# A graph attention layer and a graph transformer layer: head groups outermost, layer 0 and the output projection between attention rounds, seven equal query blocks

## The chip, the core and the metric

The kernel runs on one core of one Trainium2 chip. The metric is the device time of one execution in microseconds (us), the median of several. PE is the matrix engine (PEld its weight loads), DVE the vector engine, ACT the scalar (activation) engine, POOL the GpSimd engine, and SP the engine that only issues DMAs here. Matrix products land in PSUM, all else lives in SBUF; DRAM is reached by DMA.

## The reference

There are N = 3,327 nodes with D = 128 features and a dense N x N matrix `adj` of zeros and ones, about a quarter of a per cent of them ones, the diagonal set.

```python
# layer 0: graph attention, one head
H = x @ W.T + b;  s = H @ a_s;  r = H @ a_r
e = leaky_relu(A * s + A * r.T, 0.2)
x = layernorm(x + softmax(where(A > 0, e, NEG), axis=1) @ H)
# layer 1: D = 128 heads of width h = 8, every head sees all nodes
q, k, v = ((x @ Wq.T).reshape(d, n, h), ...)
a = softmax(einsum('dnh,dmh->dnm', q, k) * d**-0.5 + adj + adj, axis=2)
x = layernorm(x + einsum('dnm,dmh->dnh', a, v).reshape(n, h*d) @ Wo.T)
```

The 128 heads of layer 1 have 3,327 x 3,327 scores each, 1.4 billion exponentials. The reshape gives head d the rows d x 3,327 onward of the flat q, k and v, so a head is a contiguous stretch of some 26 consecutive nodes' projections: the first heads need only the first rows of x after layer 0.

## The kernel before

**Layer 0 (L99 to L225).** x is loaded and turned, h = x W, r is spread over all partitions (`rb`), s is a column (`scol`). Then 26 row tiles of 128 nodes follow, each with a row block of adj of 128 x 3,327 elements. Per tile DVE checks that adj holds zeros and ones only (L176), forms (r + s) x adj (L179) and the leaky ReLU (L182); POOL makes the mask (L183); DVE adds it and takes the row maximum (L185); ACT takes the exponential (L192); PE turns the result in 26 pieces (L198), DVE and ACT copy the pieces out (L203), PE multiplies by h (L209), and DVE divides, adds x (L214) and collects the statistics (L218, L219). At the end come a square root on ACT for all tiles (L221) and the normalization (L225).

**q, k, v (L242 to L263).** Per tile there are two matmuls of 512 columns each for q, k and v. ACT rounds q and k to a short format (L243), DVE makes the remainder (L244), so q and k have a high and a low half, and DVE takes their largest magnitude (L247). SP stores all to DRAM (`qT`, `kT`, `vd`) (L251, L263). Then a flag is computed: only if all scores are small enough and adj is zeros and ones does the fast path `plain()` run, which takes no row maximum; otherwise the slow `shifted()`.

**Attention (`plain`).** Heads go in 32 groups of four. Query columns go in blocks: six of 512 and one of 256. The outer loop is over the blocks, the inner over the groups: `groups = [(g, b) for b in blocks for g in range(NG)]`. For each block the adjT columns are loaded once on POOL's queue as bf16 (`at`, L290), and ACT makes exp(2 adj) of every third key tile (`ft`, L333). For each group and block, q (`q4b`, L346), k (`k4b`, L350) and v (`v4b`, L354) are loaded by SP, so k and v come 7 times in all for each group.

Keys are in 26 tiles (key = partition x 26 + tile). A group and block has 26 **rounds**. A round makes two half tiles of scores on PE (L298, four small matmuls, one per head). Of three consecutive key tiles one is a *times* tile: ACT takes the exponential of the scores directly from PSUM (L420) and POOL multiplies by exp(2 adj) (L421). For the other two DVE adds adj to the scores (L428) and ACT takes the exponential later for all four heads at once (L395, 2,048 elements). The last two key tiles are both added ones. Four rounds later (`LAG`) PE multiplies by v (L370, eight instructions into one PSUM bank for four heads), the ninth column of v being ones, which gives the denominator. After the last key tile DVE copies the sums out (L379) and SP stores them to `oT` (L382). There are three score buffers in PSUM of two banks each and two for the sums.

PE, ACT and DVE run in the order in which the program issues (a manual schedule); POOL and SP are ordered by the compiler's own scheduler.

**Output (L572 to L598).** For each row tile SP loads 9 x 128 values per node from `oT`, DVE divides (L572, L573), PE turns (L580), DVE and ACT copy (L582), PE multiplies by Wo (L585), and the residual and the normalization follow (L587 to L595).

Of the kernel before, what the change touches and what calls it, by code (L numbers as in the profile page):

```python
# [8 lines left out]
F32 = mybir.dt.float32  # L9
# [5 lines left out]
AX = mybir.AxisListType  # L15

# [5 lines left out]
NB = 512  # L22

SAFE = 20.0


def _ap(t, offset, dims):
    return bass.AP(tensor=t.tensor, offset=t.offset + offset, ap=[list(d) for d in dims])


@with_exitstack
def kernel(
# [20 lines left out]

    nc = tc.nc
# [11 lines left out]

    blocks = []
    for n0 in range(0, N, NB):
        nb = min(NB, (N - n0 + 1) // 2 * 2)
        at = min(n0, N - nb)  # L70
        blocks.append((at, nb, n0 - at))
    HG = 4
    NG = D // HG

# [9 lines left out]
    oT = dram.tile([H1, G], F32, name="oT")  # L84

    ident = const.tile([P, P], F32, name="ident")
    make_identity(nc, ident)
    x1 = const.tile([P, NT, D], F32, name="x1")
# [3 lines left out]

    seen = const.tile([P, 3, NT], F32, name="seen")
    nc.vector.memset(seen, 0.0)
    flag = const.tile([1, 1], I32, name="flag")

    def load_rows(engine, dst, src):

        engine.dma_start(dst[:, :FULL, :], src[: FULL * P, :].rearrange("(t p) d -> p t d", p=P))  # L99
        engine.dma_start(dst[:LAST, FULL, :], src[FULL * P :, :])  # L100


    with ExitStack() as l0:
        big = l0.enter_context(tc.tile_pool(name="l0_big", bufs=1))
        xsb = big.tile([P, NT, D], F32, name="xsb")
        load_rows(nc.sync, xsb, x)
        w0 = big.tile([P, D], F32, name="w0")
        nc.scalar.dma_start(w0, w0T)
        bcol = big.tile([P, 1], F32, name="bcol")
        nc.scalar.dma_start(bcol, b0)  # L110
        ascol = big.tile([P, 1], F32, name="ascol")
        nc.scalar.dma_start(ascol, a_s)
        arcol = big.tile([P, 1], F32, name="arcol")
        nc.scalar.dma_start(arcol, a_r)
        wq = big.tile([P, H * D], F32, name="wq")
        nc.scalar.dma_start(wq, wqT.rearrange("k h c -> k (h c)"))
        wk = big.tile([P, H * D], F32, name="wk")
        nc.scalar.dma_start(wk, wkT.rearrange("k h c -> k (h c)"))
        wv = big.tile([P, D * H], F32, name="wv")
        nc.scalar.dma_start(wv, wvT.rearrange("k c h -> k (c h)"))  # L120
        nc.scalar.dma_start(wo, woT)

        ones = big.tile([1, H1], F32, name="ones")
        nc.vector.memset(ones, 1.0)
        nc.gpsimd.dma_start(vd[G : G + 1, :], ones)

        xT = big.tile([P, N], F32, name="xT")
        hT = big.tile([P, N], F32, name="hT")
        hsb = big.tile([P, NT, D], F32, name="hsb")
        rb = big.tile([P, N], F32, name="rb")  # L130
        scol = big.tile([P, NT], F32, name="scol")

        ps = l0.enter_context(tc.tile_pool(name="l0_ps", bufs=4, space=bass.MemoryType.PSUM))
        ps1 = l0.enter_context(tc.tile_pool(name="l0_ps1", bufs=2, space=bass.MemoryType.PSUM))

        def transpose_rows(src, dst):

            for t0 in range(0, NT, 4):
                ts_ = range(t0, min(NT, t0 + 4))
                pt = ps.tile([P, 512], F32, tag="mm", name="pt")  # L140
                w = 0
                for t in ts_:
                    nc.tensor.transpose(pt[:, w : w + rows[t]], src[: rows[t], t, :], ident[: rows[t], : rows[t]])
                    w += rows[t]
                nc.vector.tensor_copy(dst[:, t0 * P : t0 * P + w], pt[:, :w])

        transpose_rows(xsb, xT)
        for n0 in range(0, N, 512):
            nb = min(512, N - n0)
            ph = ps.tile([P, 512], F32, tag="mm", name="ph")  # L150
            nc.tensor.matmul(ph[:, :nb], w0, xT[:, n0 : n0 + nb], start=True, stop=True)
            nc.vector.tensor_scalar(hT[:, n0 : n0 + nb], ph[:, :nb], bcol, None, op0=ALU.add)
            pr = ps.tile([P, 512], F32, tag="mm", name="pr")
            nc.tensor.matmul(pr[:, :nb], arcol.to_broadcast([P, P]), hT[:, n0 : n0 + nb], start=True, stop=True)
            nc.scalar.copy(rb[:, n0 : n0 + nb], pr[:, :nb])
        for t in range(NT):
            r = rows[t]
            pb = ps.tile([P, 512], F32, tag="mm", name="pb")
            nc.tensor.transpose(pb[:r, :D], hT[:, t * P : t * P + r], ident)
            nc.tensor.matmul(pb[:r, D : D + 1], hT[:, t * P : t * P + r], ascol, start=True, stop=True)  # L160
            nc.vector.tensor_copy(hsb[:r, t, :], pb[:r, :D])
            nc.scalar.copy(scol[:r, t : t + 1], pb[:r, D : D + 1])

        mv = big.tile([P, NT, 2], F32, name="mv")
        nc.vector.memset(mv, 1.0)
        with ExitStack() as gat:
            ap_ = gat.enter_context(tc.tile_pool(name="gat_a", bufs=2))
            wp = gat.enter_context(tc.tile_pool(name="gat_w", bufs=1))
            tp = gat.enter_context(tc.tile_pool(name="gat_t", bufs=2))
            sp = gat.enter_context(tc.tile_pool(name="gat_s", bufs=3))  # L170
            for t in range(NT):
                r = rows[t]
                a = ap_.tile([P, N], F32, name="a")
                nc.sync.dma_start(a[:r], adj[t * P : t * P + r, :])
                e = wp.tile([P, N], F32, name="e")
                nc.vector.scalar_tensor_tensor(  # L176
                    e[:r], a[:r], 0.0, a[:r], op0=ALU.is_gt, op1=ALU.not_equal, accum_out=seen[:r, 2, t : t + 1]
                )
                nc.vector.scalar_tensor_tensor(  # L179
                    e[:r], rb[:r], scol[:r, t : t + 1], a[:r], op0=ALU.add, op1=ALU.mult  # L180
                )
                nc.vector.scalar_tensor_tensor(e[:r], e[:r], ALPHA, e[:r], op0=ALU.mult, op1=ALU.max)  # L182
                nc.gpsimd.tensor_scalar(a[:r], a[:r], 0.0, NEG, op0=ALU.is_le, op1=ALU.mult)  # L183
                mx = sp.tile([P, 1], F32, name="mx")
                nc.vector.tensor_tensor_reduce(  # L185
                    e[:r], e[:r], a[:r], 1.0, LOWEST, op0=ALU.add, op1=ALU.max, accum_out=mx[:r]
                )
                nm = sp.tile([P, 1], F32, name="nm")
                nc.vector.tensor_scalar_mul(nm[:r], mx[:r], -1.0)  # L189
                p = tp.tile([P, N], F32, name="p")  # L190
                den = sp.tile([P, 1], F32, name="den")
                nc.scalar.activation(p[:r], e[:r], AF.Exp, bias=nm[:r], scale=1.0, accum_out=den[:r])  # L192
                pT = tp.tile([P, NT, P], F32, name="pT")
                for i0 in range(0, NT, 4):
                    is_ = range(i0, min(NT, i0 + 4))
                    pp = ps.tile([P, 4, P], F32, tag="mm", name="pp")
                    for i in is_:
                        nc.tensor.transpose(pp[: rows[i], i - i0, :r], p[:r, i * P : i * P + rows[i]], ident[:r, :r])  # L198
                    copy = nc.vector.tensor_copy if (i0 // 4) % 2 else nc.scalar.copy
                    full = [i for i in is_ if rows[i] == P]  # L200
                    if full:
                        n = len(full)
                        copy(pT[:, i0 : i0 + n, :r], pp[:, :n, :r])  # L203
                    if len(full) < len(is_):
                        i = is_[-1]
                        copy(pT[: rows[i], i, :r], pp[: rows[i], i - i0, :r])
                po = ps1.tile([P, D], F32, name="po")
                for i in range(NT):
                    nc.tensor.matmul(  # L209
                        po[:r], pT[: rows[i], i, :r], hsb[: rows[i], i, :], start=(i == 0), stop=(i == NT - 1)  # L210
                    )
                rd = sp.tile([P, 1], F32, name="rd")
                nc.vector.reciprocal(rd[:r], den[:r])
                nc.vector.scalar_tensor_tensor(  # L214
                    x1[:r, t, :], po[:r], rd[:r], xsb[:r, t, :], op0=ALU.mult, op1=ALU.add
                )
                st = sp.tile([P, 6], F32, name="st")
                nc.vector.bn_stats(st[:r], x1[:r, t, :])  # L218
                nc.vector.bn_aggr(mv[:r, t, :], st[:r])  # L219
# [419 lines left out]
```

## Time and profile before

| | us |
|---|---|
| median of 3 runs | 12,036.66 (12,035.51 to 12,043.38) |
| the profiled execution, its own time | 12,038.34 |
| its span, first to last instruction | 12,036.6 |
| busy PE / DVE / ACT / POOL | 11,035 / 9,677 / 10,238 / 8,419 |
| mean granted PE clock | 0.908 of full |
| DMA | 727.9 MB, mean 60 GB/s |

The span is cut by what each stage issues. Layer 0 ends near 905 us, the q/k/v stage near 1,260; the first add of attention starts at 1,343. The six blocks of 512 columns start at about 1,343, 2,887, 4,433, 5,982, 7,529 and 9,077, the one of 256 at 10,619, the output at 11,900. In a list of groups a row has the line, engine, operation, output <- inputs, shapes and count, then total busy time and mean ns of one, then the engine's idle time before these and what ended it. A row of windows has start:end, length, and per engine the busy time with the number of instructions, then the granted clock, the share of DMA time and GB/s. A row of the timeline has start and duration in us first.

### The profile page before, as it was taken

The page shows a single profiled execution, that of the slowest core. Times are in us where ns is not written, and L with a number is a line of the kernel's source. Part 1 is how long each engine was busy: PE and PEld are TensorE (multiplying, and loading weights), DVE is VectorE, ACT ScalarE, POOL GpSimd, SP SyncE. Part 2 cuts the span into 40 slices and gives each one's busy share as a digit, 9 for nine tenths or more (in the row PEclk, how much of TensorE's full clock was granted, in tenths as well). Part 3 has the DMA queues.
Part 4 walks back from the last instruction along what each step waited for, and adds up shares of the span by engine and source line. Part 5 has one row for each costly group of instructions (what it writes and reads, how often), then busy time and mean ns, then how long its engine had stood idle before and what let it go on. Part 6 is the DMA issues. An engine that isn't in the chain of part 4 may idle for free.

```text
span 12036.6 us, 184261 instructions
## 1 busy us (share of the span) xinstructions
PE 11035.1 (92%) x73013; PEld 4269.1 (35%) x73013; DVE 9676.5 (80%) x9126; ACT 10238.2 (85%) x8026; POOL 8419.1 (70%) x3888
## 2 busy tenths in 40 slices
PE   3335599999999999999999999999999999999998
PEld 3332133333333333333333333333333333333334
DVE  5545488888888888888888888888888888866666
ACT  1112599999999999999999999999999999976664
POOL 3440487777787877778777878777877887765552
PEclk6668799999999999999999999999999999965556
DMA  1117211112111121111211111211111111111112
GB/s 70 51 40 228 63 55 53 52 53 63 55 53 53 54 62 56 52 54 55 62 55 52 54 55 53 63 53 54 55 52 58 54 55 52 53 58 61 59 61 82
DMA packets 373572, 727.90 MB, mean 60 GB/s; under 512 B 21360, under 2 KB 304574, under 8 KB 340701
## 3 DMA queue, kind: packets, MB, share of 16 engines
q1 hardware_dynamic: 343932, 690.00, 17.0%
q0 software_dynamic: 23888, 22.15, 1.2%
q8 instruction: 578, 9.47, 0.3%
q10 hardware_dynamic: 4880, 3.87, 0.1%
q14 instruction: 294, 2.41, 0.1%
HBM read 651.20 MB, written 86.87 MB: 61 GB/s over the span
## 4 chain that ended last, share of the span: by engine, by line
PE 74%; DVE 8%; DMA 5%; issue 3%; ACT 3%; SPq 1%; POOL 0%; another core or an unknown queue 0%; ACTq 0%; DVEq 0%; POOLq 0%
PE av L370 41%; PE scb L298 32%; DVE e L428 7%; DMA k4b<-kT 2%; ACT e L395 2%; DMA kT<-ksb 1%; ACT e L420 1%; SPq L251 1%; DMA vd<-vb 0%; PE py L585 0%; DMA o<-oT 0%; DMA q4b<-qT 0%; POOL a L183 0%; POOL e L421 0%
## 5 line engine op out<-in xcount | busy, mean ns | idle before, releaser
L428 DVE TENSOR_TENSOR e<-scb,at 128x1024 f32<-128x1024 f32 (+2 forms) x8064 | 8859.2, 1143 | 1774.5 <-PE scb L298 1529.4
L421 POOL TENSOR_TENSOR e<-e,ft 128x1024 f32<-128x1024 f32 (+1 forms) x3584 | 7968.6, 2224 | 2477.4 <-ACT e L420 1661.4
L395 ACT ACTIVATE e<-e 128x2048 f32<-128x2048 f32 (+1 forms) x4032 | 7298.9, 1810 | 196.4 <-DVE e L428 170.5
L370 PE MATMUL av<-e,v4b 128*32 128x512 f32 (+1 forms) x46592 | 6233.9, 610 | 3.5 <-ACT e L395 3.4
L298 PE MATMUL scb<-q4b,k4b 32*128 32x512 f32 (+2 forms) x23296 | 5057.8, 606 | 277.1 <-DMA k4b<-kT 201.7
L298 PEld LDWEIGHTS scb<-q4b,k4b 32*128 32x128 f32 (+1 forms) x23296 | 2882.1, 296 | 5510.6 <-DVE e L428 3053.3
L420 ACT ACTIVATE e<-scb 128x1024 f32<-128x1024 f32 (+1 forms) x3584 | 3515.6, 981 | 368.9 <-PE scb L298 365.3
L370 PEld LDWEIGHTS av<-e,v4b 128*32 128x32 f32 x46592 | 954.4, 112 | 1414.1 <-issue 1378.0
L183 POOL TENSOR_SCALAR a<-a 128x3327 f32<-128x3327 f32 (+1 forms) x26 | 385.3, 14819 | 498.6 <-DVE e L179 481.9
L198 PE MATMUL pp<-ident,p 128*128 128x128 f32 (+2 forms) x676 | 133.2, 383 | 567.9 <-ACT p L192 537.3
L192 ACT ACTIVATE p<-e,nm 128x3327 f32<-128x3327 f32 (+1 forms) x26 | 79.7, 3067 | 588.2 <-DVE nm L189 588.2
L198 PEld LDWEIGHTS pp<-ident,p 128*128 128x128 f32 (+2 forms) x676 | 125.9, 210 | 574.4 <-ACT p L192 542.2
L185 DVE CUSTOM_DVE_ANT_0 e<-e,a 128x3327 f32<-128x3327 f32 (+1 forms) x26 | 94.2, 3625 | 288.2 <-POOL a L183 288.2
L333 ACT ACT_TABLE_LOAD x1 | 1.3, 1283 | 206.8 <-DMA q4b<-qT 206.8
L256 POOL MEMSET vb<- 128x128 f32 x26 | 8.6, 330 | 240.8 <-DMA vd<-vb 180.4
L209 PE MATMUL po<-hsb,pT 128*128 128x128 f32 (+2 forms) x1352 | 157.0, 277 | 0.0
L379 DVE COPY o<-av 128x512 f32<-128x512 f32 (+1 forms) x224 | 144.4, 645 | 13.9 <-PE av L370 13.7
L209 PEld LDWEIGHTS po<-hsb,pT 128*128 128x128 f32 (+2 forms) x1352 | 155.4, 194 | 0.0
L203 ACT COPY pT<-pp 128x512 f32<-128x512 f32 (+1 forms) x104 | 52.6, 506 | 120.3 <-PE pp L198 119.5
L176 DVE SCALAR_TENSOR_TENSOR e<-a 128x3327 f32<-128x3327 f32 (+1 forms) x26 | 93.8, 3607 | 32.3 <-DMA a<-in_adj_dram 32.3
L290 POOL DMA_DIRECT2D at<-in_adjT_dram x14 | 14.7, 1054 | 148.7 <-DMA vd<-vb 126.6
L342 POOL MEMSET v4b<- 128x92 f32 x224 | 39.6, 177 | 107.7 <-PE av L370 86.9
(85 smaller groups left out, 1151.8 us busy)
## 6 DMA issues: line engine op xcount, KB each, us to landing
k4b<-kT SPq DMA_DIRECT2D x896, 415.9 KB
v4b<-vd SPq DMA_DIRECT2D x224, 468.0 KB
q4b<-qT SPq DMA_DIRECT2D x1536, 32.0 KB
a<-in_adj_dram SPq DMA_DIRECT2D x25, 1663.5 KB
qT<-qsb SPq DMA_DIRECT2D x50, 512.0 KB
kT<-ksb SPq DMA_DIRECT2D x50, 512.0 KB
at<-in_adjT_dram POOLq DMA_DIRECT2D x6, 2912.0 KB, 67.1
vd<-vb SPq DMA_DIRECT2D x25, 576.0 KB
```

What stands on the lines that cost most here:

```text
L183: nc.gpsimd.tensor_scalar(a[:r], a[:r], 0.0, NEG, op0=ALU.is_le, op1=ALU.mult)
L185: nc.vector.tensor_tensor_reduce(e[:r], e[:r], a[:r], 1.0, LOWEST, op0=ALU.add, op1=ALU.max, accum_out=mx[:r])
L198: nc.tensor.transpose(pp[: rows[i], i - i0, :r], p[:r, i * P : i * P + rows[i]], ident[:r, :r])
L209: nc.tensor.matmul(po[:r], pT[: rows[i], i, :r], hsb[: rows[i], i, :], start=(i == 0), stop=(i == NT - 1))
L251: nc.sync.dma_start(_ap(dst, half * H * G + t * P * D, [[D, r], [G, H], [1, D]]), sb[:r, half, :].bitcast(F32).rearrange("p (h c) -> p h c ...
L298: nc.tensor.matmul(dst, k4[32 * j : 32 * j + H4, i::NT], q4[32 * j : 32 * j + H4, :nb], start=True, stop=stop,)
L370: nc.tensor.matmul(s.av[32 * j : 32 * j + 32, : s.nb], s.v4[:r, j, i * H1 : i * H1 + 32], e[:r, j, : s.nb], start=(s.left == NT - 1), stop ...
L379: nc.vector.tensor_copy(o4[:, : s.nb], s.av[:, : s.nb])
L395: nc.scalar.activation(e, e, AF.Exp, scale=2.0)
L420: nc.scalar.activation(eh, x[:r, :, :nb], AF.Exp, scale=2.0)
L421: nc.gpsimd.tensor_tensor(eh, eh, f[:r, i // 3, :nb].unsqueeze(1).to_broadcast([r, 2, nb]), op=ALU.mult,)
L428: nc.vector.tensor_tensor(eh, x[:r, :, :nb], a[:r, i, :nb].unsqueeze(1).to_broadcast([r, 2, nb]), op=ALU.add,)
```

## The change

The fast path becomes one program, `special()`, in which all five engines follow the order of issue. It always runs; only when its flag says no does `general()`, the old way with `shifted()`, run after it.

- **Blocks.** Seven blocks of 476 columns (`NB` = 480, `WB` = 476); the last starts 5 columns early.
- **Order.** Groups are outermost, blocks inside: k and v are loaded once per group, halfway through the last block of the group before, q once per group and block.
- **adj.** It no longer stays in SBUF for a block. At the start POOL's queue copies adjT from DRAM to DRAM, as bf16 and in the order of use (`atd`); the factors exp(2 adj) = (e^2 - 1) adj + 1 are made by DVE and stored (`ftd`), for block 0 at the start, for blocks 1 to 6 during group 0. In attention both are streamed by SP for three rounds at a time, four such stretches ahead (`AHEAD`), in six buffers.
- **Layer 0, factored.** exp(leaky_relu(s + r)) divided by exp(s) is max(exp(0.2 r) t, exp(r)) with t = exp(-0.8 s). ACT computes the three vectors once, at the start. A tile then needs on DVE a tensor_scalar per key tile (`weigh`), a multiplication by adj > 0 (`mask`), and a check of adj (`count`), and on PE 26 products with h and a column of ones. There is no transpose, no maximum, and no exponential per tile.
- **Pieces.** Layer 0 of a tile, its q/k/v projection (evicted by DVE only) and the output projection of a tile are lists of small pieces (46 and 11). Tile 0 runs at the start. The tiles that group g + 1 reads are handled during group g, in its first three quarters; the output of tiles whose heads are complete follows after them. A piece is issued after a round whose number has reached its due value. The last tile's output comes at the end. The square root is an integer first guess and three Newton steps on DVE.
- **PSUM.** One bank for the pieces, one for the sums (there were two), six for scores as before. ACT does only attention's exponentials after the start.
- **Flag.** The bound on the scores comes from the norms of the weights' columns, not from q and k; it also asks that exp(r) and t are in range.

The diff cut to its core (the loops in `general` and `shifted` are the old ones):

```diff
-NB = 512
+NB = 480
+SAFE = 40.0
+AHEAD = 4
-            groups = [(g, b) for b in blocks for g in range(NG)]
+    NBLK = max(2, -(-N // NB))
+    WB = -(-N // (2 * NBLK)) * 2
+    blocks = [(min(b * WB, N - WB), b * WB - min(b * WB, N - WB)) for b in range(NBLK)]
+            def prepare(b, pool):
...
+                        nc.vector.tensor_scalar(f, f, E2 - 1.0, 1.0, op0=ALU.mult, op1=ALU.add)
+            def layer0(t):
...
+                    def weigh(c0, c1, n=n, i0=i0):
...
+                        for i in range(c0, c1):
+                            nc.vector.tensor_scalar(
+                                s["w"][:, i - i0, :r], s["t"][:, :r], ear[:, i : i + 1], er[:, i : i + 1],
+                                op0=ALU.mult, op1=ALU.max,
+                            )
+                    def mask(c0, c1, n=n, i0=i0):
+                        a, w = (v[:, c0 - i0 : c1 - i0, :r] for v in (s["a"][n], s["w"]))
+                        nc.vector.scalar_tensor_tensor(w, a, 0.0, w, op0=ALU.is_gt, op1=ALU.mult)
+                    def count(c0, c1, k, n=n, i0=i0):
...
+                        nc.vector.scalar_tensor_tensor(
+                            a, a, 0.0, a, op0=ALU.is_gt, op1=ALU.not_equal, accum_out=odd[:, t, k : k + 1]
+                        )
+                    def products(c0, c1, i0=i0, n=n):
...
+                        for i in range(c0, c1):
+                            nc.tensor.matmul(s["p"][:r, : D + 1], s["w"][: kr[i], i - i0, :r], hsb[: kr[i], i, :],
+                                start=(i == 0), stop=(i == NT - 1))
+                units += [finish, variance, root, scale, turn, keep_turned]
...
+                def high(dst, i, scale):
+                    s["hi"] = bg2.tile([P, 512], F32R, name="hi")
+                    nc.vector.tensor_scalar(s["hi"][:r], s["b"][:r], scale, None, op0=ALU.mult)
+                    store(dst, 0, i, s["hi"])
...
+                def divided(h0):
+                    o = s["o"]
+                    nc.gpsimd.tensor_tensor(
+                        o[:r, h0 : h0 + 4, :], o[:r, h0 : h0 + 4, :],
+                        o[:r, H, :].unsqueeze(1).to_broadcast([r, 4, D]), op=ALU.mult,
+                    )
...
+            def open_adj(b, n):
+                a = ap_.tile([P, 2, WB], BF16, name="at")
+                k = len(pairs_[n])
+                nc.sync.dma_start(a[:, :k, :], atd[b][n, :, :k, :])
+                f = None
+                if n < NTR:
+                    f = ap_.tile([P, WB], F32, name="ft")
+                    nc.sync.dma_start(f, ftd[b][n])
+                return a, f
...
+                for u in range(len(side)):
+                    if u < early:
+                        due[u] = u * (total // 4) // early
+                    elif u < before:
+                        lo = total // 4 if early else 0
+                        due[u] = lo + (u - early) * (total * 3 // 4 - lo) // (before - early)
+                    else:
+                        lo = min(max(total // 8, LAG + 2, due[before - 1] + 1 if before else 0), total - 1)
+                        due[u] = lo + (u - before) * (total - 1 - lo) // (len(side) - before)
...
+                        if n % 3 == 0:
+                            m = (g * NBLK + b) * NPR + n // 3
+                            want_adj(m + AHEAD)
+                            a, f = adjs.pop(m)
+                        if n == NR // 2:
+                            if b + 1 < NBLK:
+                                queries = open_queries(g, b + 1)
+                            elif g + 1 < NG:
+                                group = open_group(g + 1)
+                                queries = open_queries(g + 1, 0)
...
+                        while len(waiting) > LAG + (n == LAG):
+                            products(*waiting.pop(0))
+                        while u < len(side) and due[u] <= at:
+                            side[u]()
+                            u += 1
...
+    special()
     fine = nc.values_load(flag[0:1, 0:1])
-    with tc.If(fine > 0) as which:
-        plain()
-    with which.Else():
-        shifted()
+    with tc.If(fine < 1):
+        general()
```

## The prediction

> **What bounds the kernel now.** I read the clock line of the page first, then the stage windows (busy time of each engine, granted clock), then the instruction groups by shape, then the waits inside one query block, then PE's timeline where its clock changes.
>
> ```profile
> core 0: us, PE busy (x) PEld busy (x) DVE busy (x) ACT busy (x) POOL busy (x), PEclk, DMA share, GB/s
> 905.00:1260.00 355.00, 157.43 (x341) 61.01 (x341) 152.82 (x222) 72.61 (x131) 7.94 (x24) 0.81 0.67 197
> 1345.00:2886.00 1541.00, 1529.60 (x9948) 567.23 (x9948) 1361.96 (x1182) 1516.97 (x1088) 1225.95 (x545) 0.99 0.16 53
> 10640.00:11895.00 1255.00, 1251.13 (x9764) 414.00 (x9756) 762.09 (x1158) 849.14 (x1064) 641.16 (x531) 0.50 0.17 58
> 11900.00:12036.00 136.00, 83.00 (x624) 74.66 (x624) 90.00 (x208) 25.34 (x54) 0.00 (x0) 0.84 0.45 127
> ```
>
> The first 1,343 us (layer 0, q/k/v, the wait for the first loads) and the last 137 us (output projection) hold no attention. A 512-column block over all 32 head groups takes some 1,541 us: ACT is busy 1,517 of them, DVE 1,362, POOL 1,226. PE's 1,530 count matmuls that wait in its pipe, so the bound is ACT. The waits in the block from 5,985 to 7,528 us agree: ACT idles 19 us behind the adds and 6 us behind the scores. The last block has half the columns and still takes 1,281 us: clock 0.50, PE always busy, ACT idle for a third. So 12,036.6 = 1,343 + 9,276 (six blocks) + 1,281 + 137.
>
> ```profile
> L428 DVE TENSOR_TENSOR e<-scb,at 128x1024 f32<-128x1024 f32 x6528 | 7675.3, 1219 | 1285.0 <-PE scb L298 1042.0 <-DMA q4b<-qT 203.4 <-POOL e L421 10.7
> L421 POOL TENSOR_TENSOR e<-e,ft 128x1024 f32<-128x1024 f32 x3072 | 7317.1, 2382 | 1919.0 <-ACT e L420 1530.0 <-POOL e L421 383.2 <-DMA oT<-o 0.3
> L428 DVE TENSOR_TENSOR e<-scb,at 128x512 f32<-128x512 f32 x1088 | 724.7, 689 | 481.6 <-PE scb L298 479.6
> L421 POOL TENSOR_TENSOR e<-e,ft 128x512 f32<-128x512 f32 x512 | 651.5, 1275 | 558.4 <-issue 292.8 <-ACT e L420 131.4 <-DVE e L428 114.7
> L333 ACT ACTIVATE ft<-at 128x4096 f32<-128x4096 bf16 x6 | 21.6, 3606 | 0.0
> L333 ACT ACTIVATE ft<-at 128x2048 f32<-128x2048 bf16 x1 | 1.9, 1894 | 0.0
> L225 DVE TENSOR_SCALAR x<-x,mv,rstd 128x128 f32<-128x128 f32 x25 | 6.5, 347 | 0.0
> ```
>
> From these pairs of shapes come the slopes: ACT (3,606-1,894)/2,048 = 0.836 ns per column, DVE (1,219-689)/512 = 1.035, POOL (2,382-1,275)/512 = 2.16.
>
> **Attention with seven equal blocks.** One group in one 512-column block takes 1,541/32 = 48.16 us. ACT sees 26 x 4 x columns per partition there; 36 columns fewer are 3,744 elements, 3.13 us. So 476 columns take 45.03 us, and 7 x 32 = 224 of them 10,087 us. This takes the place of 9,276 + 1,281 = 10,557. The gain is the last block's: at equal efficiency its 256 columns would have cost some 830 us, not 1,281.
>
> **What moves beside attention.** DVE's own 42.56 us per group and block shrink by 36 adds x 36 x 2 x 1.035 ns and a little copy to 39.8. It has 5.2 us left per block, 36.6 per group, 0.20 per round of the 26. Into this go, for each of 26 row tiles:
> - weigh: 26 of L225's shape; there 26 took 6.75 us: 6.8
> - mask, 4 pieces of 3,328 elements in all; L182 took 3.62, three more starts at 0.15: 4.0
> - count, likewise, with accumulator reads of 0.08: 4.4
> - finish, variance, root (12 tiny ones, L189 at 0.14), scale, turned copy: 3.4
> - q, k, v evictions, 10 of 512 columns at 0.68 (L244, L262): 6.8
> - result: reciprocal 0.94, two copies 0.66, the statistics, a root: 5.0
>
> Together 30.4 us per tile, nominally within 36.6. But in the first three quarters of a group layer 0's 25.4 meet only 27.4 of slack, and the pieces are lumpy. How much lag is absorbed shows at each block's end: rounds 23 to 25 have six adds (7.0 us at the 1.16 seen back to back) against three exponentials (5.4), then the copy of 0.65; ACT idles 24 us in 32 groups, 0.75 each. So about 1 us of lag is absorbed, and 3 rounds between pieces give back 0.6. Of a piece above 0.6 us, 0.6 is hidden: 29 pieces, 17.4 us, plus 1.5 of short ones, 19 in all.
>
> The term I know least is how DVE instructions that work on SBUF alone go beside L421. L428 has one operand in PSUM and runs at 1.22 us beside it; the only two-input SBUF instruction beside a POOL one is L182 (3.62 us) over the start of L183 (14.8 us), always together, so neither shows what it takes alone. Bounds: nothing, or each of 16 such pieces per tile (weigh 4, mask 4, count 4, root 2, scale 2) waits for a whole L421 at 476 columns, 2,382 - 72 x 2.16 = 2.23 us: 0 to 36 us per tile. L421 fills 35.7 of 45 us, so a piece that arrives at any moment waits 0.79 x 1.1 = 0.88 us: 14 us, the row's own mean, is my value. Loss per tile: 30.4 + 14 - 19 = 25.4 us; times 26, 660 us (bounds 296 and 1,232).
>
> [...]
>
> PE gains 52 product instructions (5.8 us, as at L209), 12 projection instructions (0.61 each, L242) and the output's 24 (3.1): 16.5 us per tile. Its shortest 512 round is 1.60 us, at 476 columns 1.53, against 1.73 of ACT: 38 us per group of cover. If ACT stopped being the bound, these would count in full, 430 us. POOL gains two half multiplies (1.28 each) and memsets over its 9 us per block. ACT gains nothing; its layer-0 exponentials, copies and q/k scaling go.
>
> DMA: at and ft are 4.1 MB per group and block, q 0.24, in 45 us 97 GB/s; k and v now come once per group, 7 GB/s more. Before, 53 GB/s took a share of 0.16, and 197 GB/s are seen in the q/k/v stage, so the loads fit. SP has some 230 issues per group at 0.65 us (q4b pairs take 1.3), 150 of 315 us; each store waits for its DVE piece, with the adj loads behind it. They are issued 12 rounds ahead, 21 us, against a k4b landing 1.7 us after its issue (6,035.3 to 6,037.05). I cost SP nothing; without this lead each late load would stall all engines by its delay.
>
> **Ends.** Start: x, transposes and h took until 50 us before; the first tile is 25 us of DVE, 14 of PE and their hand-overs, 50; loads for group 0 between 11 (15 issues and a landing) and 131 (last v store wait at 1,212 to the first add at 1,343), I take 100, since seven blocks of adj now convert at that time too. 200 us; bounds 110 and 330 (if POOL's own work waits behind seven conversions, each 45 us by the 67 us landing of 3.3 MB at L290). End: only tile 25 is left; its load and chain took 11,992 to 12,036.6: 45 us.
>
> **Sum.** 200 + 10,087 + 660 + 45 = 10,992 us of span; the profiled run lay 1.7 us over its span (12,038.3, median 12,036.7), so 10,994.
>
> **Rivals.**
> - Everything fits into slack: 10,332. Against: DVE at 98% of ACT's pace. 7 in 100.
> - No waiting behind L421: 10,628. For: L428 shows none. 25 in 100.
> - The forecast: 42 in 100.
> - DVE becomes the bound, each piece waiting for a whole L421: 11,564. 15 in 100.
> - **PE stays at half clock.** This is the case that ends slower. The trace has it:
>
> ```profile
> 2942.61 1.94 PE L370 MATMUL av<-e,v4b 128*32 128x512 f32 x8
> 2945.21 1.94 PE L370 MATMUL av<-e,v4b 128*32 128x512 f32 x8
> 2951.61 1.06 PE L370 MATMUL av<-e,v4b 128*32 128x512 f32 x8
> 10656.58 1.08 PE L370 MATMUL av<-e,v4b 128*32 128x256 f32 x8
> 10658.11 1.08 PE L370 MATMUL av<-e,v4b 128*32 128x256 f32 x8
> ```
>
> After a wait of some 4 us for k4b the clock fell to 0.50 in both. At 512 columns it was back after three rounds; at 256 it stayed for 1,240 us. A slow round takes 2.60 and 1.53 us, so 4.18 ns per column and 0.46 fixed: 82% and 70% of it streams, at 476 columns 81%, 2.45 us a round, 63.7 a block. That is 18.7 over 45.0; from 25% of attention at half clock (1,043 of 4,189 us) the change loses; all of it gives about 14,500 us. For it: DVE pieces make new gaps on PE. Against: 476 lies by the case that recovers. 7 in 100.
>
> [...]
>
> - The safety flag fails and the general path runs as well: far above 20,000 us, the old layer 0 and a slower attention. The bounds (scores under 40, adj of zeros and ones, exponents under 20) are wide for these inputs. Together with unforeseen stalls, 4 in 100.
>
> **Numbers.** Range 10,450 to 11,700: from the no-wait case with a shorter start to the whole-wait case with a longer one; outside lie 7 + 7 + 4. Faster by over 0.2% (what a measurement of this kernel can tell): 0.88; within: 0.01; slower: 0.11.
>
> **What would show it.** Right: attention starts near 200 us; a group without a tile takes 315 us, one with a tile some 340; ACT busy 93 to 95% there; its idle ends with DVE adds; clock 0.95 or more. The L421 wait: weigh, mask, or L421 itself longer than 0.26, 1.0 and 2.23 us. Wrong: SP or DMA ending ACT's waits, clock well below 0.9, a second stage after the first (flag), or a start beyond 330 us.

## The result and the profile after

The changed kernel takes **12,633 us** (median of 4 runs, 12,606 to 12,664; before 12,038 beside it). The ratio is 1.0495, 95% interval 1.0471 to 1.0519: it is 4.9% slower, where 10,994 us had been predicted. The profiled run took 12,633.1 us with a span of 12,631.3.

The stage windows of after (start:end, length, busy time and count per engine, granted clock, DMA share, GB/s), in order: the start; a block without pieces; a block with layer-0 pieces; the last block of a group; the end.

```profile
0.00:194.00 194.00, 58.15 (x180) 34.79 (x180) 53.97 (x111) 10.45 (x17) 47.52 (x77) 0.67 0.82 155
1997.30:2045.20 47.90, 46.77 (x320) 18.11 (x318) 40.65 (x40) 44.73 (x35) 35.67 (x17) 0.96 0.31 94
4192.00:4254.00 62.00, 52.74 (x329) 18.23 (x327) 54.22 (x57) 45.66 (x35) 37.98 (x17) 0.83 0.24 73
4839.60:4903.70 64.10, 49.98 (x316) 18.33 (x314) 40.12 (x39) 44.81 (x35) 35.99 (x19) 0.84 0.38 114
12578.00:12631.00 53.00, 6.26 (x28) 4.91 (x24) 6.15 (x20) 0.00 (x0) 2.48 (x2) 0.55 0.06 16
```

The start is as short as forecast. ACT's work per block is the same everywhere, 45 us (its rows overlap a little). But even a block without pieces takes 47.9 us, not 45.0. The third block has 17 DVE instructions more, 13.6 us more DVE time, and is 14 us longer. The fourth has no more work than the second and is 16 us longer. The granted clock is 0.96 where nothing is late and 0.83 and 0.84 in the two long blocks. Over attention as a whole it is 0.91:

```profile
306.70:12578.40 12271.70, 11114.48 (x71782) 4127.83 (x71782) 10064.52 (x10423) 10047.92 (x7576) 8074.49 (x3721) 0.91 0.33 99
```

The trace's clock records know only 1.00 and 0.50 here; some 2,090 of these 12,272 us are at 0.50, in stretches of at most 27 us. So a slow clock is one more rival for a part of the added time, unless it only follows the waits.

The groups answer to the rows of before (total busy and mean ns of one, then idle time):

```profile
L767 DVE TENSOR_TENSOR e<-scb,at 128x952 f32<-128x952 f32 x7616 | 8392.6, 1142 | 2128.0 <-PE scb L131 1175.3 <-DMA at<-atd 377.9 <-issue 350.9
L763 POOL TENSOR_TENSOR e<-e,ft 128x952 f32<-128x952 f32 x3584 | 8042.8, 2246 | 4328.9 <-ACT e L762 3844.2 <-issue 321.7 <-DMA ft<-ftd 79.6
L250 DVE TENSOR_SCALAR w<-tb,ear,er 128x128 f32<-128x128 f32 x650 | 454.7, 767 | 50.7 <-DMA tb<-td 50.7
L185 DVE SCALAR_TENSOR_TENSOR rsq<-st,rsq 128x1 f32<-128x1 f32 x150 | 128.1, 854 | 5.4
L423 DVE TENSOR_SCALAR x<-x,st 128x128 f32<-128x128 f32 x25 | 58.1, 2323 | 0.0
L311 DVE TENSOR_SCALAR x<-x,st 128x128 f32<-128x128 f32 x25 | 9.1, 363 | 0.0
```

The add and the multiplication have the durations that the slopes gave (1.14 and 2.25 us). The pieces do not: a weighing instruction takes 0.77 us, and a root instruction on one element per partition (L185) 0.85. L423 and L311 have the same form and differ by two microseconds. The timeline of one root shows why; DVE first, then POOL over the same time:

```profile
2134.98 1.58 DVE L185 SCALAR_TENSOR_TENSOR rsq<-st,rsq 128x1 f32<-128x1 f32 x1
2136.97 2.06 DVE L185 SCALAR_TENSOR_TENSOR rsq<-st,rsq 128x1 f32<-128x1 f32 x1
2139.45 0.22 DVE L185 SCALAR_TENSOR_TENSOR rsq<-st,rsq 128x1 f32<-128x1 f32 x1
```

```profile
2134.32 2.22 POOL L763 TENSOR_TENSOR e<-e,ft 128x952 f32<-128x952 f32 x1 [4.67 <-ACT e L762]
2136.80 2.23 POOL L763 TENSOR_TENSOR e<-e,ft 128x952 f32<-128x952 f32 x1 [0.26 <-DVE rsq L186]
```

The first two end when L763 ends (2,136.54 and 2,139.03), the third finds POOL idle. Since pieces are issued at fixed rounds, one line nearly always meets POOL (L423) and another seldom (L311). A weighing takes 338 ns in the median and 2,412 at most.

SP's queue at a change of group (start, time in issue), in the last block of group 11:

```profile
4851.86 2.67 SPq L620 DMA_DIRECT2D k4b<-kT  x4
4859.70 8.85 SPq L625 DMA_DIRECT2D v4b<-vd  x3
4868.65 22.06 SPq L637 DMA_DIRECT2D q4b<-qT  x8
4890.81 0.36 SPq L646 DMA_DIRECT2D at<-atd  x1
```

```profile
4869.00:4890.00 21.00, 10.48 (x72) 4.04 (x72) 10.84 (x10) 11.27 (x9) 7.39 (x4) 0.84 0.13 54
```

The window of those 22 us has 54 GB/s at a DMA share of 0.13, two sixteenths. The adj loads behind q4b come 39 us after the k issues, and ACT waits 14.8 us in one piece.

At the start of a block PE makes up the products held back for the sums' bank, and ACT waits for scores behind them (PE, then ACT):

```profile
1999.74 3.01 PE L668 MATMUL av<-e,v4b 128*32 128x476 f32 x16
2002.68 0.61 PE L131 MATMUL scb<-q4b,k4b 32*128 32x476 f32 x4
```

```profile
2003.41 0.96 ACT L762 ACTIVATE e<-scb 128x952 f32<-128x952 f32 x1 [2.23 <-PE scb L131]
```

**Theory.** Four separate costs are supposed: the sums' single bank, the pieces' own work, their waits for POOL, and DMAs of a form that few engines carry. The rivals: the pieces simply exceed DVE's slack, whatever POOL does; the queue's order or the bytes, not the form, make the group change late; PE's clock, not what it waits for, makes the blocks long.

### The profile page after: what moved, and what is told of

It reads as the page before. It is cut to its first block, busy times and chain, and to the rows that moved or that the text cites. A ratio compares the mean times of both kernels' runs of the same rounds, so it can differ in the third digit from the quotient of the medians.

```text
span 12631.3 us, 190034 instructions
## 1 busy us (share of the span) xinstructions
PE 11249.0 (89%) x72317; PEld 4187.1 (33%) x72317; DVE 10182.4 (81%) x10605; ACT 10111.3 (80%) x7633; POOL 8168.5 (65%) x3819
## 5 line engine op out<-in xcount | busy, mean ns | idle before, releaser
L763 POOL TENSOR_TENSOR e<-e,ft 128x952 f32<-128x952 f32 x3584 | 8042.8, 2246 | 4328.9 <-ACT e L762 3844.2
L767 DVE TENSOR_TENSOR e<-scb,at 128x952 f32<-128x952 f32 (+1 forms) x8064 | 8856.7, 1142 | 2128.1 <-PE scb L131 1175.3
L692 ACT ACTIVATE e<-e 128x1904 f32<-128x1904 f32 x4032 | 7209.5, 1788 | 829.9 <-DVE e L767 805.4
L668 PE MATMUL av<-e,v4b 128*32 128x476 f32 x46592 | 6343.4, 623 | 1.1 <-ACT e L692 1.1
L131 PE MATMUL scb<-q4b,k4b 32*128 32x476 f32 (+1 forms) x23296 | 5159.9, 608 | 1231.5 <-DVE e L767 808.2
L762 ACT ACTIVATE e<-scb 128x952 f32<-128x952 f32 x3584 | 3439.1, 960 | 1567.3 <-PE scb L131 1429.4
L250 DVE TENSOR_SCALAR w<-tb,ear,er 128x128 f32<-128x128 f32 (+1 forms) x676 | 476.1, 772 | 54.0 <-DMA tb<-td 54.0
L273 PE MATMUL bank<-hsb,w 128*128 128x129 f32 (+2 forms) x1352 | 222.3, 298 | 58.6 <-DVE w L261 58.6
L273 PEld LDWEIGHTS bank<-hsb,w 128*128 128x128 f32 (+2 forms) x1352 | 173.8, 194 | 241.8 <-issue 182.1
L677 DVE COPY o<-av 128x476 f32<-128x476 f32 x224 | 144.2, 644 | 12.4 <-PE av L668 11.9
L185 DVE SCALAR_TENSOR_TENSOR rsq<-st,rsq 128x1 f32<-128x1 f32 (+1 forms) x156 | 129.4, 829 | 5.6
L407 PEld LDWEIGHTS bank<-wo,a 128*128 128x128 f32 (+1 forms) x416 | 51.9, 196 | 47.6 <-issue 46.4
```

Source lines behind the costliest of these rows:

```text
L131: nc.tensor.matmul(dst, k4[32 * j : 32 * j + H4, i::NT], q4[32 * j : 32 * j + H4, :nb], start=True, stop=stop,)
L185: nc.vector.scalar_tensor_tensor(z, y, ve, y, op0=ALU.mult, op1=ALU.mult)
L250: nc.vector.tensor_scalar(s["w"][:, i - i0, :r], s["t"][:, :r], ear[:, i : i + 1], er[:, i : i + 1], op0=ALU.mult, op1=ALU.max,)
L273: nc.tensor.matmul(s["p"][:r, : D + 1], s["w"][: kr[i], i - i0, :r], hsb[: kr[i], i, :], start=(i == 0), stop=(i == NT - 1),)
L668: nc.tensor.matmul(s.av[32 * j : 32 * j + 32, :], s.v4[:r, j, i * H1 : i * H1 + 32], e[:r, j, :], start=(s.left == NT - 1), stop=(s.left = ...
L677: nc.vector.tensor_copy(o4, s.av)
```

## The experiments

Times are medians; the interval is that of the ratio to before. Block times are read from the distance of DVE's copies of the sums; the table has medians over the groups. The last four columns have the k loads split as well.

| us per block | after | no mult | weigh PSUM | k split | no hold | all mended | out, 1 bank | out, 2 banks |
|---|---|---|---|---|---|---|---|---|
| block 0 | 55.8 | 50.8 | 53.1 | 54.0 | 59.9 | 52.9 | 47.6 | 45.1 |
| block 1 | 62.2 | 51.5 | 57.3 | 62.1 | 61.7 | 55.8 | 47.6 | 45.2 |
| block 2 | 53.5 | 53.6 | 52.9 | 53.3 | 53.1 | 55.3 | 47.6 | 45.1 |
| block 3 | 49.1 | 49.1 | 50.3 | 49.1 | 48.8 | 48.7 | 47.7 | 45.2 |
| block 4 | 51.8 | 51.8 | 51.0 | 51.8 | 49.7 | 49.7 | 47.6 | 45.2 |
| block 5 | 47.2 | 47.0 | 47.2 | 47.4 | 46.3 | 46.5 | 47.6 | 45.2 |
| block 6 | 65.4 | 65.0 | 65.1 | 58.1 | 55.9 | 55.9 | 47.7 | 45.2 |

**1. Without POOL's multiplication** (L763; the kernel leaves out this part of the computation).

```diff
-    nc.gpsimd.tensor_tensor(eh, eh, f[:r].unsqueeze(1).to_broadcast([r, 2, WB]), op=ALU.mult)
```

> The kernel after without POOL's multiplication by exp(2 adj) (L763; this part of the computation is left out, for every third key tile). Theory A, DVE's pieces on SBUF operands wait for the POOL instruction that runs: the weighing instructions (767 ns mean) fall to 0.27 us, the root's three-operand ones (854 ns) to 0.22, the output's scale (2,323 ns) to 0.36; blocks with pieces take 48 to 52 us instead of 49 to 62; time 11,900 to 12,100. Rival B, the pieces are simply too much for DVE's slack, whatever POOL does: those durations stay within 10%, time within 1% of 12,633. Rival C, the waits are real but hidden: durations fall, time within 1%. Under all three the last block of each group stays at 65 to 72 us.

12,145 us, 1.0084 [1.0064, 1.0104]: 488 below after. The groups of DVE:

```profile
L250 DVE TENSOR_SCALAR w<-tb,ear,er 128x128 f32<-128x128 f32 x650 | 177.4, 344 | 53.8 <-DMA tb<-td 52.7 <-PE bank L273 1.1
L185 DVE SCALAR_TENSOR_TENSOR rsq<-st,rsq 128x1 f32<-128x1 f32 x150 | 32.9, 219 | 5.4
L423 DVE TENSOR_SCALAR x<-x,st 128x128 f32<-128x128 f32 x25 | 8.4, 337 | 0.0
```

All three are back at their undisturbed length, so the waits are POOL's. The time fell by less than the expected 530 to 730: only blocks 0 and 1 gained (5.0 and 10.7 us); 2 to 4 stayed. Those have another cause.

**2. k loads split.**

```diff
-    nc.sync.dma_start(k4[32 * j : 32 * j + H4, :]..., _ap(kT, d * N, [[0, 2], [G, 2 * H], [1, N]]))
+    for again in range(2):
+        nc.sync.dma_start(k4[32 * j + 16 * again : 32 * j + 16 * again + 16, :]..., _ap(kT, d * N, [[G, 2 * H], [1, N]]))
```

> The kernel after with each head's k load as two DMAs of 16 rows, in place of one whose source repeats the 16 rows with an outermost dimension of two. Theory A, that form keeps only two of the 16 DMA engines busy (53 GB/s at a DMA share of 0.13) and everything behind it on SP's queue is late: the rate right after the k issues rises above 150 GB/s, the q issues behind them no longer take 21 us, the last block of a group falls from 65 to 72 us to 48 to 52; time 12,633 - 31 x 18 = 12,080, between 12,000 and 12,250. Rival B, the bytes or the queue order are what is slow, not the form: last blocks and time within 0.5% of 12,633.

12,195 us, 1.0129 [1.0113, 1.0146]: 438 lower. SP's queue in the same block of group 11, and the window of the first ten microseconds:

```profile
4681.28 3.66 SPq L621 DMA_DIRECT2D k4b<-kT  x8
4689.12 1.57 SPq L626 DMA_DIRECT2D v4b<-vd  x3
4691.01 10.49 SPq L638 DMA_DIRECT2D q4b<-qT  x8
```

```profile
4681.00:4691.00 10.00, 10.00 (x74) 4.10 (x72) 8.64 (x9) 10.00 (x9) 8.75 (x6) 1.00 1.00 150
```

The same bytes now fill the engines (150 GB/s), the issues from k to the next adj load take 20 us instead of 39, and this block takes 47.5 us instead of 64.1. The form was the cause, not the order. Where the output's pieces lie in the last block it still takes 58; without them 47.5. The DMA share is 1.00 where it was 0.13; why a repeat of two outermost holds it there is not shown.

The kernel before loads k in the same form, and its trace had the cost already. SP issues the fourth k load of a group at 6,012.18; at 6,031.99 it begins with the next group's, of which the one at 6,035.33 is the second; PE's wait for the fourth ends at 6,037.05 (SP, then PE):

```profile
6012.18 0.61 SPq L350 DMA_DIRECT2D k4b<-kT  x1
6035.33 0.61 SPq L350 DMA_DIRECT2D k4b<-kT  x1
```

```profile
6037.05 0.73 PE L298 MATMUL scb<-q4b,k4b 32*128 32x512 f32 x1 [2.82 <-DMA k4b<-kT]
```

So a k load took some 25 us there too. Issued 21 us before the block that needs it, it held PE up for 2.8 us, and SP had no adj to stream behind it.

**3. Catching up one head per round** over four rounds, in place of a whole tile in one:

```diff
-    waiting.append((s, order[n]))
-    while len(waiting) > LAG + (n == LAG):
...
+    waiting += [(s, order[n])] * 4
+    while len(waiting) > 4 * LAG + (max(0, 2 * LAG - n) if n >= LAG else 0):
```

> The kernel after, with the products that are held back while the single bank for the sums is copied out caught up one head (two instructions) more per round over four rounds, in place of a whole tile in one round. Theory A, the burst of 16 product instructions (3.05 us) at the start of each block delays the next scores and leaves ACT idle 2.3 us: undisturbed blocks fall from 46.5 to 48.0 us to 45 to 45.7; time lower by 224 x 2 = 450 us, 12,100 to 12,350. Rival B, the bank costs by the wait for the copy itself, not by the burst: blocks and time within 0.5%.

12,937 us, 1.0743 [1.0725, 1.0761]: 304 **slower**, against both theories. PE's timeline shows what was missed:

```profile
2033.25 1.78 PE L668 MATMUL av<-e,v4b 128*32 128x476 f32 x10
2034.96 0.60 PE L131 MATMUL scb<-q4b,k4b 32*128 32x476 f32 x4
```

Eight instructions, two for each of four heads, take 1.00 us; ten take 1.78. A fifth head alone costs 0.78, where four together take 1.00, so the catching up cost 3.1 us of PE (four times 0.78) in place of the burst's 2.0 (3.01 less 1.00). That is 1.1 us per block, some 250 of the 304; no run shows the rest.

**4. t in PSUM for the weighing.**

```diff
-    nc.sync.dma_start(s["t"][:, :r], _ap(td, t * P, [[0, P], [1, r]]))
+    nc.sync.dma_start(s["t1"][:, :r], td[:, t * P : t * P + r])
...
+    s["t"] = s["p"][:, 256 : 256 + P]
+    nc.tensor.matmul(s["t"][:, :r], onerow, s["t1"][:, :r], start=True, stop=True)
```

> The kernel after, with t spread over the partitions by a one-row matmul into free columns of the piece bank (in place of a DMA into SBUF), so that the weighing instructions have one operand in PSUM; one DMA less of 64 KB, one matmul of 128 columns more per tile. Theory A, a DVE instruction with its operand in PSUM doesn't wait for POOL: the 676 weighing instructions fall from 0.77 us to 0.27 to 0.35, DVE gains 300 us, and since they lie in blocks where DVE is behind, time falls by 250 to 330 to about 12,330. Rival B, the per-partition scalars or the SBUF output are what waits: durations within 10%, time within 0.5%. Rival C, durations fall but the blocks are held by something else: time within 0.5%.

12,396 us, 1.0296 [1.0279, 1.0313]: 238 lower, a little less than expected. The weighing no longer waits (400 ns in the mean, 767 in after), but the mask behind it, with two SBUF inputs, now takes 1.90 and 1.82 us (942 and 1,133 ns in after); that it meets POOL there is inferred from these lengths:

```profile
L256 DVE TENSOR_SCALAR w<-bank,ear,er 128x128 f32<-128x128 f32 x650 | 215.6, 400 | 56.6 <-PE bank L252 44.4 <-PE scb L131 12.2
L267 DVE SCALAR_TENSOR_TENSOR w<-a,w 128x768 f32<-128x768 f32 x50 | 94.9, 1898 | 0.1
L267 DVE SCALAR_TENSOR_TENSOR w<-a,w 128x896 f32<-128x896 f32 x50 | 91.0, 1820 | 0.1
```

Of the 252 us of DVE that the operand's place won, 82 were lost again in the mask.

**5 and 6. The pieces outside attention**, with one and with two banks for the sums. Core of the edit (k split as well; the second has `bufs=2` for `pv` and no holding back):

```diff
-                for u in first:
-                    u()
+                run(tiles, 24)          # all 26 tiles, two at a time, own buffers and banks
...
-                        side += layer0(t)
...
-                        side += result(t)
...
+            run([result(t) for t in range(NT)], 4)     # after attention
```

> The kernel after with the k loads split, with all layer-0 and q/k/v tiles before attention (pipelined, with buffers and PSUM banks of their own, q/k high halves and v copied out by ACT) and all outputs after it; still one bank for the sums. It tells what the pieces cost inside attention. Theory A, nearly all of a piece's work is added to the blocks: all blocks but the last of a group take 46.5 to 48 us, the last 48 to 52; attention 224 x 47 + 31 x 3 + some 40 for group 0's conversions = 10,660; the tiles before it by DVE 25 x 21.5 = 540, by DMA some 115 MB at 197 GB/s = 585, so the first scores at 800 to 950; output 140; time 11,600 to 11,800. Rival B, the blocks that have pieces are long for another reason (DMA, adj streaming): blocks 0 to 4 keep a mean near 53, time above 12,600.

> As the one before, with the bank that the pieces had given to the sums again (two banks, and no product round held back at a block's start). Theory A, a single bank costs 2 us or more per block: blocks fall to 45.0 to 45.5 us, time 224 x 2 = 450 below the one before, 11,050 to 11,350. Rival B, undisturbed blocks are longer than 45.0 for another reason (the streamed adj, six buffers): the two agree within 0.5%.

12,084 us, 1.0033 [1.0020, 1.0045], and 11,569 us, 0.9606 [0.9590, 0.9622]. Both are some 220 to 280 us above their expected ranges: the blocks are as expected, the two ends were longer (first block's end at 1,145, output 304). With one bank a block takes 47.6 us and no block stands out (but for the conversions in group 0), so what made the others long was the pieces, by their work, their waits or the slow clock that comes with them. The second bank, together with the end of holding back, is worth 515 us, 2.3 per block, and gives the forecast pace: 45.2 against 45.03, with a granted clock of 1.00 in attention against 0.96 with one bank. The streamed adj costs nothing that shows. The start held a surprise, stores of the last tile's 127 rows, each blocking the queue for 12 us at a share of 0.07, one sixteenth (this is with two banks):

```profile
948.41 11.93 SPq L336 DMA_DIRECT2D kT<-lo  x1
```

```profile
912.00:984.00 72.00, 0.21 (x1) 0.01 (x1) 1.26 (x10) 0.00 (x0) 0.00 (x0) 0.51 0.07 22
```

**7. Each layer-0 product twice** (L273).

```diff
+    for again in range(2):
         nc.tensor.matmul(s["p"][:r, : D + 1], s["w"][...], hsb[...],
-            start=(i == 0), stop=(i == NT - 1))
+            start=(i + again == 0), stop=(i + again == NT))
```

> The kernel after with each of layer 0's 26 products per tile made twice into the same sum (numerator and denominator both double, so the result is the same): 0.94 us of PE more in each of 10 pieces per tile. Theory A, PE has no cover in a round that carries a piece (the three score buffers tie PE, DVE and ACT together): each costs 0.85 to 0.95 us, time up by 25 x 9 = 225 us, to 12,830 to 12,880. Rival B, the prediction's cover of 38 us per group holds: time within 0.3% of 12,633.

12,770 us, 1.0598 [1.0580, 1.0616]: 136 more, between the two theories' numbers. But less work was added than the expectation took. PE's rows for these products (after, then this run):

```profile
L273 PE MATMUL bank<-hsb,w 128*128 128x129 f32 (+2 forms) x1352 | 222.3, 298 | 58.6 <-DVE w L261 58.6
L274 PE MATMUL bank<-hsb,w 128*128 128x129 f32 (+2 forms) x2704 | 373.5, 287 | 58.3 <-DVE w L261 58.3
```

They grew by 151 us, not by 235 (25 tiles of 9.4): 0.94 us is the length of a piece of six instructions, and a piece of twelve takes 1.61. So some nine tenths of the added PE time show, as theory A says with too high a price per piece. With runs of one kernel up to 57 us apart the share is rough, but a cover that hides it is out.

**8. The kernel before with seven equal blocks.**

```diff
-NB = 512
+NB = 476
```

> The kernel before with nothing changed but seven blocks of 476 columns (the last of 472) in place of six of 512 and one of 256. Forecast from the trace of before: 10,087 in place of 10,557 for attention, 12,040 - 470 = 11,570; range 11,500 to 11,650 if clock and pace per column stay as at 512 columns. Rival: narrow blocks stick at half clock like the one of 256; then above 12,300.

11,680 us, 0.9697 [0.9681, 0.9713]. The mean clock rose from 0.908 to 0.957; blocks of 476 columns did not stay at half clock as the one of 256 did. The pace is 45.6 us (11,688.6 of span less 1,343 and 137, over 224), 0.5 above the slope's 45.0, which is 120 us in all and puts the time 30 us above the expected range.

**9. No holding back** (with the k split).

```diff
-    while len(waiting) > LAG + (n == LAG):
+    while len(waiting) > LAG:
```

> The kernel after with the k loads split (12,195 us by itself), and without holding the products back in round 4 of a block: PE then waits for the copy of the single bank where it stands. Theory A, the wait for the copy is shorter (1 us) than what holding back costs (2.4 us per block): undisturbed blocks 46 to 46.5 us, time 224 x 1.2 = 270 lower, about 11,930. Rival B, the copy stands behind DVE's adds, so that PE waits 2 us or more: blocks 47.6 or longer, time 12,195 to 12,400. Rival C: equal within 0.3%.

12,045 us, 1.0005 [0.9996, 1.0015]: 150 below the k split alone, about half of the expected gain. Undisturbed blocks take 45.4 to 46.3, so there PE's wait for the copy is shorter than the catching up. Block 0 became 5.9 us longer, which took back part of the gain; why is open.

**10. The 127-row DMAs cut** into 112 and 15 rows, here the stores of q and k; the others likewise.

```diff
-    nc.sync.dma_start(_ap(dst, ... + t * P * D, [[D, r], [G, 4], [1, D]]), sb[:r]...)
+    for p0, p1 in cut(r):           # (0, 128), or (0, 112) and (112, 127)
+        nc.sync.dma_start(_ap(dst, ... + (t * P + p0) * D, [[D, p1 - p0], [G, 4], [1, D]]), sb[p0:p1]...)
```

> The kernel after with every DMA of the last tile's 127 rows cut into 112 and 15 rows. Theory A, an outermost count that 16 doesn't divide keeps a DMA on few engines (seen: 256 KB of 127 rows in 11.9 us, 22 GB/s, share 0.07): only group 29, where that tile runs, and the end change: group 29 from 443 to 385 us, the end from 53 to 45; time 12,560 to 12,580. Rival B, the count doesn't matter: group 29 and the time as before within 10 us.

12,554 us, 1.0430 [1.0413, 1.0447]: 79 lower, slightly more than expected. Group 29 fell from 443 to 384 us, the end from the last copy on from 53 to 30.

**11. A version that beats both.** Pieces outside, two banks, and its ends mended: rows cut, loads of a tile issued two tiles ahead, of an output four ahead, group 0's conversions with one load ahead over 2/5 of the group.

```diff
+    tiles[k].insert(AHEAD0, lambda k=k: (loads[k + 2](), spread[k + 2]()))
...
-    due[u] = u * (total // 4) // early
+    due[u] = u * (total * 2 // 5) // early
...
+    ends[k].append(loads[k + 4])
```

> The version with the pieces outside attention and two banks for the sums (11,569 us), with four changes on its two ends: the 127-row DMAs cut (12 issues of 11.9 us each before attention: -95), a tile's loads issued two tiles ahead (DVE waits 6 us of each 30 for them: -150), the conversions of group 0 with one load ahead and spread over 2/5 of the group (-50), the output's loads four tiles ahead (11.7 us per tile, of which DVE waits 5: -110). Expected 11,100 to 11,250, blocks unchanged at 45.2 us. Rival: the DMA rate, not the order of the loads, sets the tile pace of 30 us (share 0.55): then only the rows' 95 us and some of the output's go, 11,350 to 11,450.

**11,150 us**, 0.9262 [0.9246, 0.9277], as expected: the 26 tiles run at 25 us each instead of 30, the first block ends at 861 instead of 1,144, the output takes 174 instead of 304. The DMA rate did not stand in the way: it rose from 151 to 186 GB/s.

**12. Everything mended, the pieces left inside** (edits 2, 4, 9 and 10 together).

> The kernel after with everything mended that was found, and the pieces left between the attention rounds: k loads split, 127-row DMAs cut, t in PSUM for the weighing, no holding back at a block's start. Theory A, the four are separate and add up: from 12,045 with the first and the last, less 79 for the rows and 240 for the weighing, 11,725; range 11,680 to 11,800. It stays 500 us and more above the version with the pieces outside (11,150), since a piece's work is added to the blocks nearly in full and the pieces hold a bank of PSUM. Rival B, once the waits are gone the pieces sink into the slack of DVE: below 11,500. Rival C, the weighing's gain was only a shift of phase that holding back had caused: 11,900 or more.

11,691 us, 0.9708 [0.9692, 0.9724]. The four add up (11,725 expected), and what is left is no better than experiment 8, which changes one constant.

## Why the prediction was wrong

The forecast was 1,640 us too low, and three of its steps failed. SP's loads and stores were put at nothing and cost 517 us. The sums' single bank had no term and cost 515 us with the holding back that it brings. Of each tile's pieces 19 us were to be hidden, so that all would cost 660 us; they cost some 1,140. The sum of the prediction against what the runs give, put together from several kernels:

| term | forecast | measured | from |
|---|---|---|---|
| start | 200 | 194, and 108 later in group 0 | first block 113 and group 0 436 us, against 56 and 385 |
| 224 blocks | 10,087 | 10,125 | 45.2 in experiment 6 |
| one bank for sums, with holding back | none | 515 | 5 against 6 |
| k form, 127 rows | none | 438 + 79 | 2, 10 |
| waits for POOL | 364 (14 x 26) | 488 | 1 |
| other cost of pieces | 296 (11.4 x 26) | some 656 | what the other rows leave of 12,633 |
| end | 45 | 30, and 23 in the 127 rows | 10 |

- **"I cost SP nothing", "the loads fit".** Wrong: 517 us. The rate was argued from 53 GB/s at a share of 0.16 and 197 GB/s elsewhere, as if any DMA used all engines. The 1.7 us from k4b's issue to its "landing" was misread: the wait that ended at 6,037.05 was for the load issued at 6,012.18, so the trace of before said 25 us (experiment 2). In after the adj loads stood behind k and q for 39 us, against a lead of 21.
- **One bank for the sums.** The change was described and not costed: 515 us. In the kernel with its pieces, dropping the holding back alone wins 150 of them (experiment 9). What it did to the order of PE (products held back, then 16 in a row) shows in PE's rows: 1 us idle in the round that is held, then 2 us more of products in one round.
- **"About 1 us of lag is absorbed ... 19 in all".** Wrong. Blocks 2 to 4 lengthen without POOL too. DVE's free 5 us per block are not at a piece's disposal: a round uses two of the three score buffers, so DVE, ACT and PE wait for each other in a ring, and a delay of one is passed on. This mechanism is argued from the waits and not shown by itself; the 656 us, 25 us per tile where 11.4 was forecast, are a remainder, in which whatever does not add up lies too.
- **"PE: 38 us per group of cover".** Wrong: some nine tenths of added PE time show (136 of 151 us, experiment 7).
- **The wait behind L421.** Right in kind and near in size, in part by luck: 14 us per tile forecast, 19 measured (488/26; whatever else the multiplication delays is in it). The forecast let four of the 16 waits of a tile be the weighing's. There are 26 weighings, which wait 0.42 us each on average (767 less 344 ns), 11 us per tile by themselves, while the mask hardly waits (942 and 1,133 ns, against 947 and 1,079 without POOL).
- **Half clock.** This rival, the only one that ended slower but for the flag, came about in part: a sixth of attention, where it asked for a quarter to lose by itself. By its own price, 18.7 us lost in 63.7, the 2,090 us at half clock would be up to 610 us, an estimate, and would lie inside the rows above, the remainder most of all. How much of that the clock causes stays open: the mean over attention rises with each wait that is taken away (0.93 with k split, 0.94 without POOL's multiplication, 0.96 with the pieces outside, 1.00 with the second bank), so it may only follow. Its "about 14,500" for half clock throughout is 15,180 by its own terms (10,994 and 4,189), unless the pieces' 660 are then hidden.
- **Equal blocks, the start.** Right: 45.2 us a block, first add at 198.4. The forecast's 45.03 started from a window of 1,541 us; 9,276 over 192 is 48.31 in place of 48.16, which is the difference. The 360 us that equal blocks bring by themselves were real; the rest of the change cost 950 (12,633 against 11,680).
- The rival "whole-L421 waits", 11,564, was the nearest one, and it too lacked the DMAs and the bank.

## What to carry to other kernels

Here an engine's free share was no measure of what work put between the rounds of a pipeline with a short ring of buffers would cost: such pieces cost more inside (some 44 us per tile, 488 and 656 us over 26) than in a stage of their own (25 us, and 6.7 for the output), and with both sides mended the kernel with them inside takes 11,691 us against 11,150. Before moving loads, look at the DMA share beside the rate: here a share of 0.07 or 0.13 stood beside an outermost count of 127 or 2, and the split of the latter brought 1.00. A resource that a change takes away, such as a bank, is a term of the sum like any instruction.

## What the runs showed of the hardware that was not expected

- A DMA with 127 rows outermost moved 22 GB/s at a share of 0.07, one with a repeat of two outermost 54 GB/s at 0.13; cut or split, the same transfers took less time: the split k loads moved 150 GB/s at a share of 1.00, and the cut rows took 79 us off the kernel.
- A three-operand DVE instruction on one element per partition took 0.22 us alone and up to 2.2 us beside a POOL multiplication, to whose end it waited; with its tensor operand in PSUM, a weighing took 0.40 us and did not wait.
- Eight product instructions, for four heads into four partition groups, took 1.00 us, ten 1.78: a lone head cost 0.78 us, three quarters of a full set.
- The granted clock over attention was 0.91 in the kernel after and 1.00 in the version with two banks and the same shapes, and half clock never lasted longer than 27 us in the former. In the kernel before, blocks of 256 columns stayed at 0.50 for 1,240 us with PE busy 1,251 of 1,255 us.
